# Reordering the set-up of a fused conv, state-space, attention and expert kernel

## The chip, the cores and the metric

The kernel runs on one core of a Trainium2 chip. The metric is the device time of one execution in microseconds (us), as the median of several runs. A core has TensorE (matmuls, PE in the profile), VectorE (DVE), ScalarE (ACT), GpSimd (POOL) and SyncE (SP). Transfers between device memory and on-chip memory (DMA) are issued from the queues of SyncE or ScalarE here and carried by 16 DMA engines.

## The reference, cut to what matters

The input x has 4 images of 128 channels and 64 x 64 pixels, in float32.

```python
x = x + conv_block(gn(x))           # layer 0
t = to_tokens(x)                    # (4, 4096, 128)
t = t + attention(ln(t))            # layer 1, 4 heads of 32
t = t + experts(ln(t))              # 8 experts, the best 2 of each token
out = from_tokens(t)

def gn(v, G=32, eps=1e-5):          # statistics over 4 channels and all pixels
    g = v.reshape(B, G, C // G, H, W)
    return ((g - mean(g)) / sqrt(var(g) + eps)).reshape(v.shape)

def conv_block(x):
    xn = ln(x)                                        # over channels
    h = depthwise_3x3(xn) + fc1_b
    y = xn + fc2(gelu(ln(h))) + fc2_b
    chunks = ln(y) split into 4 groups of 32 channels
    m = mamba(chunks) + skip * chunks                 # a scan over 4096 pixels, 16 states
    return ln(xn + cat(m)) @ proj_w.T + proj_b
```

Group normalisation needs the mean and variance of a whole image before its first block can be normalised. Some weights are prepared once. The expert and router weights and the projection are centred over the channels, so that the mean of a normalisation need not be subtracted later. Norms of the query, key and value weights bound the attention scores: the flag `general` says whether a slower general attention must run after all, which is decided at the kernel's end.

## The kernel before, in words

An image is cut into NB = 8 blocks of 512 pixels (8 rows of 64), with the 128 channels on the partitions. The kernel has two parts.

The **set-up** (L59 to L193) loads weights with `load` (L53 to L57), on SyncE's queue unless another is given, makes constants, prepares weights and computes the bound. Its order on each engine comes from a scheduler that follows the data and the order of the program. The tiles `taps` (nine diagonal matrices of the depthwise weights, L85 to L87), `inxc` (L90 to L93), `amat`, `wdt` and `crow` are made here. The pools `scratch` and `bound` are closed at its end, and the memory is given to the main pools.

The **main part** is written out by hand, in slots. The helper `Queue` (L467 is the line in it that records every operation of this part) chains the instructions of each engine in the order of the program. Work on blocks runs as generators in two lanes, X and Y, which `advance` moves on by one stage. `until` (L1246 on) runs the lanes until a named piece is done; it is what works off the first blocks, before slot 0 can start. For each image the lanes run:

- `group_norm(b)`: loads all eight blocks of the image (`xg`), takes bn_stats of each, then the group means with two small matmuls by `gmat`, and `gr`, the power -1/2 of the variance, on GpSimd;
- `first_norm(b, i)`: loads a block again (`gn`), normalises it with the group's mean `gm` and `gr`, transposes it, normalises each pixel over the channels (statistics on VectorE, power on GpSimd, scaling on ScalarE, the tile `xt`), transposes back and writes `y0` with a border; block i also writes the last border row of block i - 1;
- `conv(b, i)`: nine taps of the depthwise convolution (on TensorE for image 0, on VectorE for the others), normalisation, gelu, the matmul `fc2T`, the sum with y0, normalisation again, giving `xn`; then `pairs`, a shifted copy, goes through a transfer;
- `inputs(b, i, p)`: projections, silu and softplus for half p of the channels; it writes `bc` to memory, to be fetched as broadcast `rows`.

The slots of the main loop then run the scans on VectorE (`h`), read them out (`hc`), sum over states with transposing matmuls (`y`), and interleave attention (`sc`, `pT`, `av`) and experts (`share`).

```python
    mix, att, side = pool("mix"), pool("att"), pool("side")
...
    for k in range(2):
        gpsimd.memset(decays[k][:, 0, BLK:], 0.0)
```

The first statement lays out the main pools in memory. The memset (tile `da`) is the first instruction of the main part on GpSimd.

Of the kernel before, what the change touches and what calls it, by code (L numbers as in the profile page):

```python
# [9 lines left out]
F32 = mybir.dt.float32  # L10
# [26 lines left out]
def conv_mamba_attn_moe_kernel(ctx: ExitStack, tc: tile.TileContext, t: dict):  # L37
# [20 lines left out]

    ident = const.tile([P, P], F32, name="ident")  # L59
# [10 lines left out]
    gmat = load("gmat")  # L70
    lnw, lnb, lcw, lcb = (load(k) for k in ("lnw", "lnb", "lcw", "lcb"))
    fc1w, fc1b, fc2T, fc2b = (load(k) for k in ("fc1w", "fc1b", "fc2T", "fc2b"))
    inz, cb, dtb, dsk, wbc = (load(k) for k in ("inz", "cb", "dtb", "dsk", "wbc"))
    wout, projT = (load(k) for k in ("wout", "projT"))
    wv, wp, rw, ew, eb8 = (load(k, eng=nc.scalar) for k in ("wv", "wp", "rw", "ew", "eb8"))
    wqn, wkn, bqn, bkn = (load(k, eng=nc.scalar) for k in ("wqn", "wkn", "bqn", "bkn"))
# [3 lines left out]
    inx, xdt, dtT, alog = (load(k, pool=scratch) for k in ("inx", "xdt", "dtT", "alog"))  # L80
    bvc, bp = (load(k, pool=scratch) for k in ("bvc", "bp"))
    cw = load("cw", [P, 4, P], t["cw"].partition_broadcast(P), pool=scratch)
# [20 lines left out]
    with (  # L103
        tc.tile_pool(name="bound", bufs=1) as bd,
        tc.tile_pool(name="ps_w", bufs=2, space=PSUM) as ps_w,
    ):
# [3 lines left out]
        pw = ps_w.tile([P, P], F32, name="pw")  # L110
        nc.tensor.matmul(pw[0:1, :], lhsT=bvc, rhs=wp, start=True, stop=True)
        crow1 = bd.tile([1, C], F32, name="crow1")
        nc.vector.tensor_add(crow1, pw[0:1, :], bp)
        pw = ps_w.tile([P, P], F32, name="pw")
        nc.tensor.matmul(pw, lhsT=ones, rhs=crow1, start=True, stop=True)
        nc.vector.tensor_copy(crow, pw)

        sq = bd.tile([P, 2 * NH + 1], F32, name="sq")
        nc.vector.memset(sq, 0.0)
        bsq = bd.tile([DH, 2 * NH], F32, name="bsq")
        for i, (w, bias) in enumerate(((wqn, bqn), (wkn, bkn))):
            for h in range(NH):
                r = slice(DH * h, DH * h + DH)
# [516 lines left out]
    def conv(b, i):  # L643
        cm = tmp("Y", "cm")
        h = work("Y") if b == 0 else cm
        hr = h.rearrange(IMAGE, w=IMG)

        def tap(k):
            y0 = y0_rows(b, i, k // 3, k % 3)
# [837 lines left out]
```

## Time and profile before

| What | us |
|---|---|
| Median of 3 runs | 5233.21 (5232.01 to 5235.14) |
| The profiled execution's own time | 5221.24 |
| Its span in the profile | 5219.4 |
| PE busy | 4743.5 (91%) |
| VectorE busy | 3834.5 (73%) |
| ScalarE busy | 3749.8 (72%) |
| GpSimd busy | 423.5 (8%) |
| First scan input (`h`) starts at | 98.11 |

Busy times are of the profiled execution. PE's is an overestimate of its use, since its matmuls are pipelined and their ends modelled. Times in the timeline count from the start of the span. "Idle before" an instruction is followed by what released it. L467 stands for the whole main part, so its groups are told apart by the names of their tiles.

### The profile page before, as it was taken

What the parts mean: (1) busy time and instruction counts of PE and PEld (TensorE: products, weight loads), DVE (VectorE), ACT (ScalarE), POOL (GpSimd) and SP (SyncE); (2) the same over time, 40 slices, a digit from 0 to 9 for tenths busy, and PEclk for the clock granted to TensorE, in tenths of its full rate; (3) what the DMA queues carried; (4) which work ended last, traced back from release to release, by engine and by line L of the source; (5) the groups of instructions that cost most, each with busy time, mean ns of one, the idle gap of its engine ahead of it and who ended that gap; (6) DMA issues with size and microseconds to landing.
All of it is one profiled execution on the core that took longest, in us unless ns stands there. A gap on an engine that the chain in (4) does not pass through costs nothing.

```text
span 5219.4 us, 62693 instructions
## 1 busy us (share of the span) xinstructions
PE 4743.5 (91%) x20704; PEld 2300.7 (44%) x20704; DVE 3834.5 (73%) x5809; ACT 3749.8 (72%) x5701; POOL 423.5 (8%) x483
## 2 busy tenths in 40 slices
PE   4566898999999999899999999999999999999997
PEld 2333444444444444444444444444444444443443
DVE  4888767777788877888788877888788877751332
ACT  3456787788777777688887787788777787756543
POOL 1111101100000000001000000000000001000000
PEclk8677999999999999899999999999999999999998
DMA  3556667767776667767766667767766666754542
GB/s 96 188 186 202 206 215 247 232 231 238 244 231 218 227 227 243 238 232 246 260 230 231 224 223 230 262 227 259 259 236 227 215 230 226 263 181 153 184 134 72
DMA packets 451694, 1131.62 MB, mean 217 GB/s; under 512 B 51985, under 2 KB 135330, under 8 KB 451362
## 3 DMA queue, kind: packets, MB, share of 16 engines
q1 hardware_dynamic: 450194, 1126.74, 64.3%
q8 instruction: 166, 2.72, 0.2%
q14 instruction: 166, 1.36, 0.1%
q10 hardware_dynamic: 1168, 0.80, 0.1%
HBM read 967.12 MB, written 143.39 MB: 213 GB/s over the span
## 4 chain that ended last, share of the span: by engine, by line
PE 55%; DVE 18%; ACT 13%; DMA 6%; issue 5%; POOL 2%; SPq 1%; DVEq 0%; ACTq 0%; POOLq 0%
PE av L467 23%; PE sc L467 13%; PE ps_X L467 8%; DVE h L467 6%; PE ps_Y L467 5%; PE y L467 5%; ACT pT L467 4%; ACT L467 3%; DMA ks<-kd 2%; DVE hc L467 2%; ACT xt L467 1%; ACT e L467 1%; DMA rows<-bcd 1%; DVE stX L467 1%; POOL rsX L467 1%
## 5 line engine op out<-in xcount | busy, mean ns | idle before, releaser
L467 ACT ACTIVATE pT<-sc 128x1024 f32<-128x1024 f32 x2048 | 1984.8, 1023 | 940.1 <-PE sc L467 938.4
L467 PE MATMUL av<-pT,v 128*64 128x512 f32 x8192 | 1998.3, 609 | 12.4 <-DVE avs L467 12.4
L467 PE MATMUL sc<-qs,ks 128*128 128x512 f32 x4096 | 1296.1, 436 | 64.4 <-DMA ks<-kd 32.7
L467 DVE TENSOR_TENSOR_SCAN h<-da,state,h 128x1025 f32<-128x1025 f32 x512 | 1204.2, 2352 | 90.0 <-ACT h L467 56.2
L467 PEld LDWEIGHTS sc<-qs,ks 128*128 128x128 f32 x4096 | 701.3, 190 | 793.3 <-ACT pT L467 261.7
L467 PEld LDWEIGHTS av<-pT,v 128*64 128x64 f32 x8192 | 499.5, 137 | 844.4 <-issue 813.8
L467 ACT ACTIVATE da<-delta,amat 128x512 f32<-128x512 f32 x1024 | 743.0, 730 | 1.9
L467 PE MATMUL y<-ident,hc 128*128 128x128 f32 x4096 | 626.6, 284 | 64.9 <-DVE hc L467 64.9
L467 DVE TENSOR_TENSOR hc<-rows,h 128x1024 f32<-128x1024 f32 x512 | 624.2, 1219 | 16.1 <-PE y L467 5.9
L467 DVE TENSOR_TENSOR h<-rows,du 128x1024 f32<-128x1024 f32 x512 | 623.4, 1218 | 14.2 <-DMA rows<-bcd 13.7
L467 PEld LDWEIGHTS y<-ident,hc 128*128 128x128 f32 x4096 | 520.6, 147 | 235.7 <-issue 83.9
L467 ACT ACT_TABLE_LOAD x319 | 409.3, 1283 | 19.5 <-DVE zs L467 14.3
L467 POOL TENSOR_TENSOR rsX<-rsX,mhalf 128x4 f32<-128x4 f32 x92 | 203.8, 2216 | 2524.6 <-DVE rsX L467 2440.5
L467 POOL TENSOR_TENSOR rsY<-rsY,mhalf 128x4 f32<-128x4 f32 x100 | 130.4, 1304 | 2071.0 <-DVE shiftY L467 1560.3
L467 DVE TENSOR_TENSOR avs<-av,prev 128x512 f32<-128x512 f32 x96 | 66.1, 689 | 252.9 <-PE av L467 238.3
L467 PE MATMUL ps_X<-share,w_ew 128*128 128x512 f32 x432 | 215.5, 622 | 8.7 <-DVE share L467 8.5
L467 ACT ACTIVATE xt<-ps_Y,shiftY,rsY 128x128 f32<-128x128 f32 x380 | 143.8, 469 | 106.4 <-POOL shiftY L467 99.0
L467 DVE TENSOR_TENSOR share<-share,xf 128x1024 f32<-128x1024 f32 x128 | 155.9, 1218 | 15.6 <-DMA share<-sharesX 9.9
L467 ACT COPY state<-h 128x2 f32<-128x2 f32 x448 | 88.7, 198 | 93.5 <-DVE h L467 93.5
L467 DVE SCALAR_TENSOR_TENSOR cm<-y,w_fc1w,cm 128x512 f32<-128x512 f32 x192 | 142.8, 744 | 3.4
L467 PE MATMUL ps_Y<-pairs,inxc 128*128 128x512 f32 x256 | 129.2, 629 | 15.6 <-DMA pairs<-xn 10.3
L467 PEld LDWEIGHTS ps_X<-share,w_ew 128*128 128x128 f32 x432 | 73.6, 190 | 146.8 <-issue 98.5
(254 smaller groups left out, 3455.8 us busy)
## 6 DMA issues: line engine op xcount, KB each, us to landing
rows<-bcd SPq DMA_DIRECT2D x1024, 512.0 KB
ks<-kd SPq DMA_DIRECT2D x192, 512.0 KB
qs<-qd SPq DMA_DIRECT2D x161, 512.0 KB
share<-sharesX SPq DMA_DIRECT2D x108, 512.0 KB
v<-vd SPq DMA_DIRECT2D x192, 256.0 KB
ks<-kd SPq DMA_DIRECT2D x128, 256.0 KB
avd<-avs SPq DMA_DIRECT2D x96, 256.0 KB
prev<-avd SPq DMA_DIRECT2D x96, 256.0 KB
```

The lines of the kernel that those rows point to most:

```text
L467: return lambda *args, **kw: queued(op(*args, **kw))
```

## The change

- Eight tiles `x0` in `scratch` take the eight blocks of image 0; their loads are the first on SyncE's queue.
- All weights but `rb`, `skip` and `projb` are loaded from ScalarE's queue, in a new order. `bvc` and `bp` move from `scratch` to `const`.
- The group statistics of image 0 are computed in the set-up, from `x0`; `group_norm(0)` is no longer put into lane Y.
- The bound check, `crow` and the centring leave the set-up for a generator, `prepared_weights`. `until` moves it on by one stage per round once y0 of block 1 has been issued; what is left is run in slot 0. It works in a `pT` tile of the attention and in the PSUM tile `av`. The eight Gram matrices share one PSUM tile, as do their squares, and `ew` is centred in two matmuls of 512 columns instead of eight of 128.
- The convolution of block (0, 0) does taps 0 to 4 on TensorE and taps 5 to 8 on VectorE, and adds the two sums on VectorE.
- The pool `att` is opened ahead of `mix`.

```diff
--- before.py
+++ after.py
@@ -56,6 +56,12 @@
         eng.dma_start(out=w, in_=src)
         return w
 
+    x0 = []
+    for i in range(NB):
+        xs = scratch.tile([P, BLK], F32, name=f"x0{i}")
+        nc.sync.dma_start(out=xs, in_=x[0][:, i * BLK : (i + 1) * BLK])
+        x0.append(xs)
+
     ident = const.tile([P, P], F32, name="ident")
     make_identity(nc, ident)
     ones = const.tile([1, P], F32, name="ones")
@@ -67,19 +73,19 @@
     for e in range(NE):
         nc.gpsimd.memset(rev[:, e : e + 1], float(NE - e))
 
-    gmat = load("gmat")
-    lnw, lnb, lcw, lcb = (load(k) for k in ("lnw", "lnb", "lcw", "lcb"))
-    fc1w, fc1b, fc2T, fc2b = (load(k) for k in ("fc1w", "fc1b", "fc2T", "fc2b"))
-    inz, cb, dtb, dsk, wbc = (load(k) for k in ("inz", "cb", "dtb", "dsk", "wbc"))
-    wout, projT = (load(k) for k in ("wout", "projT"))
-    wv, wp, rw, ew, eb8 = (load(k, eng=nc.scalar) for k in ("wv", "wp", "rw", "ew", "eb8"))
-    wqn, wkn, bqn, bkn = (load(k, eng=nc.scalar) for k in ("wqn", "wkn", "bqn", "bkn"))
+    late = nc.scalar
+    gmat, fc1w = (load(k, eng=late) for k in ("gmat", "fc1w"))
+    inx, xdt, dtT, alog = (load(k, pool=scratch, eng=late) for k in ("inx", "xdt", "dtT", "alog"))
+    cw = load("cw", [P, 4, P], t["cw"].partition_broadcast(P), pool=scratch, eng=late)
+    lnw, lnb, fc1b, lcw, lcb = (load(k, eng=late) for k in ("lnw", "lnb", "fc1b", "lcw", "lcb"))
+    fc2T, fc2b, cb, dtb, dsk = (load(k, eng=late) for k in ("fc2T", "fc2b", "cb", "dtb", "dsk"))
+    inz, wbc, wout, projT = (load(k, eng=late) for k in ("inz", "wbc", "wout", "projT"))
+    wv, wp, rw, ew, eb8 = (load(k, eng=late) for k in ("wv", "wp", "rw", "ew", "eb8"))
+    wqn, wkn, bqn, bkn = (load(k, eng=late) for k in ("wqn", "wkn", "bqn", "bkn"))
+    bvc, bp = (load(k, eng=late) for k in ("bvc", "bp"))
     rb = load("rb", [P, NE], t["rb"].partition_broadcast(P))
     skip = load("skip", [P, 1], t["skip"].partition_broadcast(P))
     projb = load("projb", [P, C], t["projb"].rearrange("o c -> (o c)").partition_broadcast(P))
-    inx, xdt, dtT, alog = (load(k, pool=scratch) for k in ("inx", "xdt", "dtT", "alog"))
-    bvc, bp = (load(k, pool=scratch) for k in ("bvc", "bp"))
-    cw = load("cw", [P, 4, P], t["cw"].partition_broadcast(P), pool=scratch)
 
 
     taps = const.tile([P, 9, P], F32, name="taps")
@@ -100,96 +106,29 @@
 
     crow = const.tile([P, C], F32, name="crow")
     general = const.tile([1, 1], I32, name="general")
-    with (
-        tc.tile_pool(name="bound", bufs=1) as bd,
-        tc.tile_pool(name="ps_w", bufs=2, space=PSUM) as ps_w,
-    ):
+    with tc.tile_pool(name="ps_w", bufs=2, space=PSUM) as ps_w:
+        gst = small.tile([P, NB, 6], F32, name="gst", bufs=1)
+        for i in range(NB):
+            nc.vector.bn_stats(out=gst[:, i, :], in_=x0[i])
+        gmv = small.tile([P, 2], F32, name="gmv", bufs=1)
+        nc.vector.bn_aggr(out=gmv, in_=gst)
+        pw = ps_w.tile([P, P], F32, name="pw")
+        nc.tensor.matmul(pw[:, 0:1], lhsT=gmat, rhs=gmv[:, 0:1], start=True, stop=True)
+        gm0 = small.tile([P, 1], F32, name="gm", bufs=2)
+        nc.vector.tensor_copy(gm0, pw[:, 0:1])
+        gd = small.tile([P, 1], F32, name="gd", bufs=1)
+        nc.vector.tensor_sub(gd, gmv[:, 0:1], gm0)
+        gv = small.tile([P, 1], F32, name="gv", bufs=1)
+        nc.vector.scalar_tensor_tensor(gv, gd, gd, gmv[:, 1:2], ALU.mult, ALU.add)
+        pw = ps_w.tile([P, P], F32, name="pw")
+        nc.tensor.matmul(pw[:, 0:1], lhsT=gmat, rhs=gv, start=True, stop=True)
+        gr0 = small.tile([P, 1], F32, name="gr", bufs=2)
+        nc.vector.tensor_scalar_add(gr0, pw[:, 0:1], EPS)
+        nc.gpsimd.tensor_tensor(gr0, gr0, mhalf[:, 0:1], ALU.pow)
+
         pw = ps_w.tile([P, P], F32, name="pw")
         nc.tensor.matmul(pw, lhsT=xdt, rhs=dtT, start=True, stop=True)
         nc.vector.tensor_copy(wdt, pw)
-        pw = ps_w.tile([P, P], F32, name="pw")
-        nc.tensor.matmul(pw[0:1, :], lhsT=bvc, rhs=wp, start=True, stop=True)
-        crow1 = bd.tile([1, C], F32, name="crow1")
-        nc.vector.tensor_add(crow1, pw[0:1, :], bp)
-        pw = ps_w.tile([P, P], F32, name="pw")
...
-        for i, (w, bias) in enumerate(((wqn, bqn), (wkn, bkn))):
-            for h in range(NH):
-                r = slice(DH * h, DH * h + DH)
-                pw = ps_w.tile([P, P], F32, name="pw")
...
-        ok = bd.tile([1, 1], F32, name="ok")
-        nc.vector.tensor_reduce(ok, fine, AX.X, ALU.min)
-        nc.vector.tensor_scalar(ok, ok, -1.0, 1.0, ALU.mult, ALU.add)
-        nc.vector.tensor_copy(general, ok)
-        cen = bd.tile([P, P], F32, name="cen")
-        nc.vector.tensor_scalar(cen, ident, 1.0 / C, None, ALU.subtract)
-
-        def centred(w, src):
...
-        centred(rw, rw)
-        ewf = ew.rearrange("p e c -> p (e c)")
-        centred(ewf, ewf)
-        gain = bd.tile([P, C], F32, name="gain")
...
-        nc.vector.tensor_add(projb, pw, projb)
-        centred(projT, gain)
     setup.close()
@@ -501,7 +440,7 @@
             tc.tile_pool(name=name, bufs=bufs, **({} if space is None else {"space": space}))
         )
 
-    mix, att, side = pool("mix"), pool("att"), pool("side")
+    att, mix, side = pool("att"), pool("mix"), pool("side")
     ps_sc, ps_av, ps_y = pool("ps_sc", 2, PSUM), pool("ps_av", 1, PSUM), pool("ps_y", 1, PSUM)
     ps_work = pool("ps_work", 1, PSUM)
 
@@ -564,6 +503,7 @@
     held = set()
     group_of, y0_of, xn_of, pairs_of, in_of, gated, kqv = {}, {}, {}, {}, {}, {}, {}
     IMAGE = "p (r w) -> p r w"
+    group_of[0] = gm0, gr0
 
     def load_x(src, i, name):
         xs = side.tile([P, BLK], F32, tag="xs", name=name, bufs=4)
@@ -643,28 +583,34 @@
     def conv(b, i):
         cm = tmp("Y", "cm")
         h = work("Y") if b == 0 else cm
-        hr = h.rearrange(IMAGE, w=IMG)
+        half = b == i == 0
 
         def tap(k):
             y0 = y0_rows(b, i, k // 3, k % 3)
             w = fc1w[:, k : k + 1]
 
-            if b == 0:
-                mm(hr, taps[:, k, :], y0, k == 0, k == 8)
-            elif k == 0:
+            hr = (cm if half and k > 4 else h).rearrange(IMAGE, w=IMG)
+            if b == 0 and not (half and k > 4):
+                mm(hr, taps[:, k, :], y0, k == 0, k == (4 if half else 8))
+            elif k == 0 or half and k == 5:
                 vector.tensor_scalar(hr, y0, w, fc1b, ALU.mult, ALU.add)
             else:
                 vector.scalar_tensor_tensor(hr, y0, w, hr, ALU.mult, ALU.add)
 
-        for k in range(0, 9, 2):
+        for k in range(0, 5 if half else 9, 2):
             if b:
                 yield
             tap(k)
-            if k < 8:
+            if k < (4 if half else 8):
                 tap(k + 1)
+            if half and k < 4:
+                tap(k + 5)
+                tap(k + 6)
             if b == 0:
                 yield
-                if k == 8:
+                if half and k == 4:
+                    vector.tensor_add(cm, h, cm)
+                elif k == 8:
                     scalar.activation(cm, h, AF.Identity, bias=fc1b)
             yield
         ps = transposed("Y", by_tile(cm))
@@ -1209,6 +1155,99 @@
         yield
 
 
+    def prepared_weights():
+
+        kept_in = att.tile([P, 2, BLK], F32, name="pT", bufs=4).rearrange("p k q -> p (k q)")
+        column = [0]
+
+        def part(n, rows=P):
+            c = column[0]
+            column[0] += n
+            return kept_in[0:rows, c : c + n]
+
+        def bank():
+            return ps_av.tile([P, BLK], F32, name="av")
+
+        cen, gain, lnbs, gv = (part(P) for _ in range(4))
+        g, sq, bsq, col1 = part(2 * NH * DH, DH), part(2 * NH + 1), part(2 * NH, DH), part(1)
+        crow1 = part(C, 1)
+        norm, bnorm, power = part(2 * NH + 1, 1), part(2 * NH, 1), part(4 * NH, 1)
+        wn, most, score, fine, ok = (part(n, 1) for n in (2 * NH, 2 * NH, NH, NH + 1, 1))
+        heads = [
+            (NH * i + h, slice(DH * h, DH * h + DH), w, bias)
+            for i, (w, bias) in enumerate(((wqn, bqn), (wkn, bkn))) for h in range(NH)
+        ]
+        gpsimd.memset(power[:, 0 : 2 * NH], 0.125)
+        gpsimd.memset(power[:, 2 * NH :], 0.5)
+        vector.memset(sq, 0.0)
+        vector.memset(col1, 1.0)
+        vector.tensor_scalar(cen, ident, 1.0 / C, None, ALU.subtract)
+        ps = bank()
+        for k, r, w, _ in heads:
+            mm(ps[0:DH, DH * k : DH * k + DH], w[:, r], w[:, r])
+        mm(ps[0:1, 2 * NH * DH : 2 * NH * DH + C], bvc, wp)
+        yield
+        vector.tensor_copy(g, ps[0:DH, 0 : 2 * NH * DH])
+        vector.tensor_add(crow1, ps[0:1, 2 * NH * DH : 2 * NH * DH + C], bp)
+        yield
+        ps = bank()
+        for k, _, _, _ in heads:
+            c = slice(DH * k, DH * k + DH)
+            mm(ps[0:DH, c], g[:, c], g[:, c])
+        mm(ps[:, 2 * NH * DH : 2 * NH * DH + C], ones, crow1)
+        for k, r, _, bias in heads:
+            vector.tensor_copy(bsq[:, k : k + 1], bias[r, :])
+        vector.tensor_mul(bsq, bsq, bsq)
+        vector.tensor_mul(gv, wv, wv)
+        vector.tensor_reduce(sq[:, 2 * NH : 2 * NH + 1], gv, AX.X, ALU.add)
+        yield
+        vector.tensor_copy(g, ps[0:DH, 0 : 2 * NH * DH])
+        vector.tensor_copy(crow, ps[:, 2 * NH * DH : 2 * NH * DH + C])
+        vector.tensor_mul(g, g, g)
+        vector.tensor_reduce(
+            sq[0:DH, 0 : 2 * NH], g.rearrange("p (k d) -> p k d", d=DH), AX.X, ALU.add
+        )
+        yield
+        ps = bank()
+        mm(ps[0:1, 0 : 2 * NH + 1], col1, sq)
+        mm(ps[0:1, DH : DH + 2 * NH], col1[0:DH, :], bsq)
+        yield
+        vector.tensor_copy(norm, ps[0:1, 0 : 2 * NH + 1])
+        vector.tensor_copy(bnorm, ps[0:1, DH : DH + 2 * NH])
+        vector.tensor_scalar(
+            fine[:, NH : NH + 1], norm[:, 2 * NH : 2 * NH + 1], VALUE_MAX, None, ALU.is_le
+        )
+        yield
+        gpsimd.tensor_tensor(wn, norm[:, 0 : 2 * NH], power[:, 0 : 2 * NH], ALU.pow)
+        gpsimd.tensor_tensor(bnorm, bnorm, power[:, 2 * NH :], ALU.pow)
+        for k in range(0, NE * C, BLK):
+            ps = bank()
+            mm(ps, cen, ew.rearrange("p e c -> p (e c)")[:, k : k + BLK])
+            yield
+            vector.tensor_copy(ew.rearrange("p e c -> p (e c)")[:, k : k + BLK], ps)
+            yield
+        vector.tensor_scalar_mul(gain, projT, lnw)
+        vector.tensor_copy(lnbs, lnb.to_broadcast([P, P]))
+        yield
+        ps = bank()
+        mm(ps[:, 0:C], lnbs, projT)
+        mm(ps[:, C : 2 * C], cen, gain)
+        mm(ps[:, 2 * C : 2 * C + NE], cen, rw)
+        yield
+        vector.tensor_add(projb, ps[:, 0:C], projb)
+        vector.tensor_copy(projT, ps[:, C : 2 * C])
+        vector.tensor_copy(rw, ps[:, 2 * C : 2 * C + NE])
+        yield
+        vector.scalar_tensor_tensor(most, wn, 1.001 * float(C) ** 0.5, bnorm, ALU.mult, ALU.add)
+        vector.tensor_mul(score, most[:, 0:NH], most[:, NH:])
+        vector.tensor_scalar(fine[:, 0:NH], score, SCORE_MAX / ATT_SCALE, None, ALU.is_le)
+        vector.tensor_reduce(ok, fine, AX.X, ALU.min)
+        vector.tensor_scalar(ok, ok, -1.0, 1.0, ALU.mult, ALU.add)
+        vector.tensor_copy(general, ok)
+        yield
+
+    weights = prepared_weights()
+
     lanes, done, running = {"X": deque(), "Y": deque()}, set(), {}
 
     inside = {"X": False, "Y": False}
@@ -1251,6 +1290,8 @@
                 advance(*half) for half in (("X", True), ("Y", False), ("Y", True), ("X", False))
             ]
             assert any(moved) or len(done) > count, key
+            if ("y0", *blocks[1]) in done:
+                next(weights, None)
 
     blocks = [(b, i) for b in range(B) for i in range(NB)]
 
@@ -1262,7 +1303,7 @@
 
     def upper(k):
         b, i = blocks[k]
-        if i == 0:
+        if i == 0 and b > 0:
             Y.append((("group", b), group_norm(b), []))
         if k != 1:
             Y.append((("y0", b, i), first_norm(b, i, "Y"), before(k, 4)))
@@ -1326,6 +1367,8 @@
         flush()
         if slot == 0:
             fetch((0, 0), (0, 1), (1, 0))
+            for _ in weights:
+                pass
             prepared(0, 0)
             prepared(0, 1)
         fetch((at + 2, 0) if odd else (at + 1, 1))
```

## The prediction

> **What bounds the kernel now.** I read the busy times by stage first (columns: length, then busy time and instructions of matmul, weight load, VectorE, ScalarE and GpSimd; granted clock, DMA share, GB/s).
>
> ```profile
> 0.00:39.00 39.00, 14.23 (x68) 10.11 (x68) 19.29 (x98) 1.50 (x2) 5.62 (x24) 1.00 0.40 110
> 39.00:98.00 59.00, 28.04 (x64) 12.95 (x65) 10.50 (x48) 21.20 (x35) 5.65 (x17) 0.79 0.10 30
> 98.00:400.00 302.00, 176.68 (x658) 105.56 (x657) 266.08 (x330) 160.78 (x316) 36.55 (x36) 0.72 0.55 186
> ...
> 1000.00:2000.00 1000.00, 948.62 (x4270) 461.64 (x4267) 798.25 (x1152) 793.44 (x1217) 84.57 (x97) 0.99 0.70 233
> ```
>
> TensorE bounds the body (95% busy); VectorE, with the scans, bounds 98 to 400 us (88%). Neither bounds the first 98 us: there no engine is half busy, and time is latency. The change touches only this stretch. So the question is how much earlier the first scan's input (L467 h, 98.11 us) is ready, and whether all that follows moves with it. Then the timeline of the set-up (start, length, engine, instruction, idle before and releaser):
>
> ```profile
> 13.56 0.33 SPq L56 DMA_DIRECT2D w_cw<-in_cw  x1
> 13.94 9.61 SPq L467 DMA_DIRECT2D xg<-in_x  x8
> ...
> 17.84 1.19 DVE L93 TENSOR_TENSOR inxc<-w_inx,w_cw 64x128 f32<-64x128 f32 x4 [2.00 <-DMA w_cw<-in_cw]
> ...
> 27.59 0.35 DVE L467 BATCH_NORM_AGGREGATE gmv<-gst 128x2 f32<-128x48 f32 x1
> ...
> 33.12 0.14 DVE L467 TENSOR_SCALAR gr<-ps_Y 128x1 f32<-128x1 f32 x1
> ...
> 37.71 0.29 DVE L180 COPY w_projT<-pw 128x128 f32<-128x128 f32 x1
> 37.87 0.14 POOL L467 MEMSET da<- 128x1 f32 x2 [5.41 <-issue]
> 37.94 0.54 POOL L467 MEMSET vst<- 128x512 f32 x1
> 38.42 0.58 POOL L467 TENSOR_TENSOR gr<-gr,mhalf 128x1 f32<-128x1 f32 x1
> 39.04 0.55 DVE L467 TENSOR_SCALAR gn<-gn,gm,gr 128x512 f32<-128x512 f32 x1 [1.04 <-POOL gr L467]
> ...
> 43.87 1.50 ACT L467 ACTIVATE xt<-ps_Y,shiftY,rsY 128x128 f32<-128x128 f32 x4 [29.54 <-POOL shiftY L467]
> ```
>
> The rows of x are asked for only at 13.94, behind 26 weight loads on the SP queue. Their statistics are interleaved with the bound check on VectorE. The group variance is there at 33.26, but its power waits on GpSimd behind a memset that starts only when the last set-up tile is written (37.71 + 0.29). The first block can start at 39.0. The waits of the SP queue show that a load can hold up later issues:
>
> ```profile
> SPq L56 <- DMA w_ew<-in_ew: 1.4, 1, 1.4
> ```
>
> Last, the first block's convolution and what follows:
>
> ```profile
> 52.68 9.67 PE L467 MATMUL ps_Y<-y,taps 128*128 128x512 f32 x18
> ...
> 54.39 0.34 PEld L467 LDWEIGHTS ps_Y<-y,taps 128*128 128x128 f32 x1 [0.52 <-issue]
> ...
> 57.47 0.19 PEld L467 LDWEIGHTS ps_Y<-y,taps 128*128 128x128 f32 x1 [0.24 <-issue]
> ...
> 62.39 0.69 ACT L467 ACTIVATE cm<-ps_Y,w_fc1b 128x512 f32<-128x512 f32 x1 [8.39 <-PE ps_Y L467]
> ...
> 70.25 2.08 PE L467 MATMUL ps_Y<-g,w_fc2T 128*128 128x512 f32 x2 [0.98 <-ACT g L467]
> ```
>
> Each tap is two passes. Their weight loads come every 0.86 us (0.34 + 0.52) at first and every 0.43 us (0.19 + 0.24) from about 56.4 us on.
>
> **What the Trainium skill says.** "TensorE: Matmul & The Clock Gate", Part 1: the clock has a half and a full state and needs some 3.4 us of activity to rise. The 0.86 and 0.43 us passes agree, although the windows print 1.00 for the same time. "DMA: Bandwidth & Descriptors", section "Issuing engines are not separate DMA queues": loads issued by ScalarE and SP share the same DMA engines, so a second queue saves only issue time. The trace agrees with sharing: the 256 KB load of cw took 4.28 us (13.56 to 17.84) beside four x loads. "ScalarE: Activation LUTs", section "What ACT_TABLE_LOAD costs": 1283 ns; the trace has 1.28.
>
> **The change part by part.** *Order.* I compared the built programs by engine. From the first input projection (inxc) on, all five engines issue the same instructions in the same order in both, with the same waits but for the now unneeded or first-use waits on loads. The swap of the pools att and mix adds none: cost 0. What changes is the first 83 us.
>
> *Loads.* 45 loads precede the first pairs transfer in both (26 + 10 on SP and 9 on ScalarE; now 13 and 32). In the built program each waits for the load eight places before it, both queues counted together. An issue takes 0.46 us; a 64 KB load (wv) landed 2.0 us after its issue, and cw 4.28. For a 256 KB x load beside others I take 3.4 us, about the mean of both. x00 is issued at 0.75 as gmat was, and lands at 4.1. On ScalarE alog waits for it (4.1) and cw follows (4.6), landing at 8.9. x03 waits for gmat (2.8) and lands with the others' data at 7.5: four x loads and cw moved 1.28 MB between 15 and 20 us before, so about 1 us per 256 KB. x07 shares cw's place, goes at 8.9 and lands at 12.3. gn follows rb, skip and projb on SP and lands near 15: before it is needed.
>
> *Statistics.* VectorE's order now is four bn_stats, inxc, two bn_stats, nine taps, two bn_stats, aggregate. cw frees inxc at 8.9; then 1.19 (inxc) + 1.34 (2 x 0.67) + 1.85 (taps row) + 1.34 + 0.35 = 6.07 gives 15.0. x07 is needed at 13.95, after it lands. Then gmat's matmul 0.58, three small VectorE rows 0.73 (28.61 to 29.34), matmul 0.58, gr 0.14, power 0.58 and 0.24 for hand-overs: 2.85. The group's gr is ready at 17.8 instead of 39.0: **21.2 us earlier**. Ends: 16.2 if loads land as fast as wv did; 20.5 if each x load takes as long as cw.
>
> *The ScalarE queue.* xt is wanted 4.87 us after gr (43.87 - 39.0), so at 22.7. dtb is the 16th of 32 loads and waits for x07 (12.3); it and the 16 after it at 0.46 end at 20.1; table load 1.28 and amat 0.22 make 21.6. So it hides, by 1.1 us. If the big loads hold the queue as ew held SP (1.4 us each, for ew, wout and cw), ScalarE is 3.1 us late: cost 0 to 3.1, I take 0.
>
> *Convolution* (times of before, from y0 on). PE first does eight 32x32 matmuls and a row: a pair of passes was 0.32 us alone, some 0.2 in a stream: 1.8 us, so taps start at 54.4. Slow clock until 56.2 (two passes), six passes at 0.43: 58.8. Then eight g matmuls and crow, 1.6; the fifth tap 0.86 and its drain: 61.4. VectorE meanwhile does tap 5 (0.55), waits for block 1's row (54.0), then tap 6, g, crow, taps 7 and 8, bsq, gv: 0.74 + 0.33 + 0.28 + 1.49 + 1.1 + 0.7 ends at 58.7, so it is covered by PE. The sum, a 0.7 us add, ends at 62.1 instead of 63.08: 1.0 saved. If the small matmuls take 0.32 each, 2 us of this go back; if PE is warm from the first tap, 1 more is won.
>
> *Check and centring in the gaps.* g, crow, square and reduction (0.33 + 0.29 + 0.33 + 0.3) stand ahead of the next bn_stats and overlap the 0.66 us transposes: +0.5. One 512-wide ew matmul precedes fc2T while ScalarE makes g: at 1.72 to 2.08 from 69.2 it ends at 70.9 or later against 70.25: +0.6. It may leave PE warm, so that fc2T's 2.08 falls by up to 0.8: I take -0.6. The w_ew copies, the second ew matmul, the last three matmuls and the small VectorE rows lie under transposes (1.12), GpSimd's power and xt (4.3 together), and the 2.3 us pairs transfer: 0. Were that last cover gone, they would cost about 2 us. GpSimd's two powers (1.67 + 1.63) come after shift and 9 us before the next one: 0.
>
> Sum: 21.2 + 1.0 - 0.5 - 0.6 + 0.6 = 21.7, rounded to **21.5 us** earlier. The body keeps its order and its waits, so nothing refills the gap; what is late next is still the scan chain, only earlier. The span would go from 5219.4 to 5197.9 and the profiled execution from 5221.24 to 5199.7. The median of the runs lies 12.0 above that execution, taken as unchanged: 5233.2 - 21.5 = **5211.7**.
>
> **Rivals.** *The ScalarE queue sets the start* (10%): 32 loads in one queue, with waits crossing to SP. For: the margin is 1.1 us and SP stalled 1.4 us on ew. Against: most of these loads are small. Gain 21.5 - 6 = 15.5 at twice the stalls: 5217.7.
>
> *TensorE gains too* (8%): the extra matmuls leave it at full clock for the taps, fc2T and inxc, two matmuls of which took 3.57 us at 83.72 where 1.72 is warm. For: PE now works in the gaps. Against: idle stretches of 2 to 4 us remain. Gain 21.5 + 0.8 + 1.8 + 2 = 26: 5207.
>
> *The head was hidden anyway* (4%): the body would wait for something not moved. For: the scans run at 88% of VectorE, not 100. Against: the chain of waits runs without a break from gn through y0, taps, xn and pairs to h. It would give 5230, inside 0.2%.
>
> *Slower: the clock sinks between 98 and 400 us* (4%). In the first 300 us matmuls of ps_Y, ps_X and y are 16.9 + 4.0 + 2.7% of the chain, 71 us, at a mean of 0.72. Loss cancels the gain where 71 x (0.72/c - 1) = 21.5, at c = 0.55; at a steady half clock it is 31 us and the time 5243. For: the windows show 0.50 at 70 to 80 and at 180 to 200 us. Against: the work between is the same.
>
> **How the numbers follow.** The main case has 74%, with its own range 5207 to 5217 from the ends of loads and convolution. Both neighbours of same sign are needed for eight in ten with margin: 5204 to 5220. About 0.2% (10.5 us) is what a measurement can tell from no change; faster by more needs half of the forecast gain, which the first three cases give: 0.92. Hidden head 0.04, slower 0.04.
>
> **What would show it.** bn_stats from about 4.5 us; the aggregate near 14.6; gr's power ending at 17 to 19; xt near 22.7; taps in two groups on PE and four rows on VectorE, the add ending near 41; the first scan input h near 76.5; every later stage shifted alike. It is wrong if the last ScalarE load is issued after 22 us, if inxc waits past 11 us for cw, if the fifth tap waits on VectorE, or if the shift at h is not the shift at the end.

## The result, and the profile after

The changed kernel took 5215.75 us (median of 6 runs, 5212.52 to 5219.71), beside 5237.89 us (6 runs, 5232.01 to 5245.92) for the kernel before. The ratio is 0.9967, with a 95% interval of 0.9954 to 0.9979: faster by 17.3 us of 5233 (11.0 to 24.1). The forecast was 21.5 us of gain and 5211.7 us. Its profiled execution took 5213.97 us with a span of 5211.8.

First the busy times by stage of the changed kernel. The stages are the same pieces of work as in the table shown for the kernel before: up to the group's power, up to the first scan input, the next 302 us, and one millisecond of the body (columns as there: length, PE, PEld, VectorE, ScalarE, GpSimd, granted clock, DMA share, GB/s).

```profile
0.00:19.50 19.50, 1.89 (x6) 1.50 (x6) 9.22 (x26) 0.00 (x0) 2.23 (x20) 1.00 0.73 183
19.50:78.40 58.90, 31.22 (x106) 15.54 (x107) 21.14 (x91) 22.09 (x36) 8.95 (x20) 0.79 0.17 43
78.40:380.00 301.60, 179.16 (x657) 106.32 (x655) 263.32 (x329) 158.90 (x313) 36.88 (x36) 0.72 0.55 185
1000.00:2000.00 1000.00, 946.58 (x4276) 460.14 (x4276) 797.39 (x1142) 796.19 (x1219) 83.23 (x96) 0.99 0.70 233
```

The first stage shrank from 39.0 to 19.5 us: VectorE now does 26 instructions in it instead of 98, and DMA runs at 0.73 of its engines instead of 0.40. The second stage kept its length (58.9 against 59.0) although VectorE has twice the work in it. The last two stages are unchanged.

The timeline of the changed kernel's head (start, length, engine, instruction, idle before and releaser):

```profile
5.06 0.36 ACTq L56 DMA_DIRECT2D w_cw<-in_cw  x1
...
10.78 1.19 DVE L99 TENSOR_TENSOR inxc<-w_inx,w_cw 64x128 f32<-64x128 f32 x4 [2.58 <-DMA w_cw<-in_cw]
...
16.25 0.37 DVE L114 BATCH_NORM_AGGREGATE gmv<-gst 128x2 f32<-128x48 f32 x1
...
18.90 0.57 POOL L127 TENSOR_TENSOR gr<-gr,mhalf 128x1 f32<-128x1 f32 x1 [16.66 <-DVE gr L126]
...
19.50 0.55 DVE L406 TENSOR_SCALAR gn<-gn,gm,gr 128x512 f32<-128x512 f32 x1 [0.76 <-POOL gr L127]
...
22.30 0.30 ACTq L56 DMA_DIRECT2D w_bp<-in_bp  x1
...
23.93 0.21 ACT L102 ACTIVATE amat<-w_alog 128x16 f32<-128x16 f32 x1
...
24.34 1.51 ACT L406 ACTIVATE xt<-ps_Y,shiftY,rsY 128x128 f32<-128x128 f32 x4 [0.20 <-POOL shiftY L406]
...
34.70 4.54 PE L406 MATMUL ps_Y<-y,taps 128*128 128x512 f32 x8
...
35.72 0.34 PEld L406 LDWEIGHTS ps_Y<-y,taps 128*128 128x128 f32 x1 [0.52 <-issue]
...
36.51 0.19 PEld L406 LDWEIGHTS ps_Y<-y,taps 128*128 128x128 f32 x1 [0.45 <-issue]
...
36.94 0.19 PEld L406 LDWEIGHTS ps_Y<-y,taps 128*128 128x128 f32 x1 [0.24 <-issue]
...
40.20 1.13 PE L406 MATMUL ps_Y<-y,taps 128*128 128x512 f32 x2
...
41.37 0.69 DVE L406 TENSOR_TENSOR cm<-ps_Y,cm 128x512 f32<-128x512 f32 x1 [2.30 <-PE ps_Y L406]
...
50.21 1.91 PE L406 MATMUL ps_Y<-g,w_fc2T 128*128 128x512 f32 x2
...
78.44 1.23 DVE L406 TENSOR_TENSOR h<-rows,du 128x1024 f32<-128x1024 f32 x1
```

The statistics' chain is closed: inxc waits 2.58 us for cw, and from there to gr's power there is nothing but work and the hand-overs between engines. GpSimd takes the power as soon as its input is there; the memset `da` now runs at 1.66 us, long before. ScalarE is only just ready for xt: its last load is issued at 22.30, amat ends at 24.14, and xt starts at 24.34, released by GpSimd. The shift of each stage against the kernel before:

| Stage | Before | After | Shift | Forecast of the shift |
|---|---|---|---|---|
| gr's power ends | 39.00 | 19.47 | 19.5 | 21.2 |
| sum of the taps ends | 63.08 | 42.06 | 21.0 | 22.2 |
| fc2T starts | 70.25 | 50.21 | 20.0 | 21.1 |
| first inxc matmul starts | 83.72 | 63.58 | 20.1 | 21.7 |
| first scan input h starts | 98.11 | 78.44 | 19.7 | 21.7 |

The two profiled executions, though, differ by only 7.6 us in span (5219.4 and 5211.8). The first experiment shows why they can't be compared at their ends.

### The profile page after: what moved, and what is told of

Same layout as the page of the kernel before. It is cut to its first block, busy times and chain, and to the rows that moved or that the text cites. A ratio compares the mean times of both kernels' runs of the same rounds, so it can differ in the third digit from the quotient of the medians.

```text
span 5211.8 us, 62608 instructions
## 1 busy us (share of the span) xinstructions
PE 4743.5 (91%) x20684; PEld 2298.3 (44%) x20684; DVE 3834.8 (74%) x5780; ACT 3749.6 (72%) x5700; POOL 423.0 (8%) x483
## 4 chain that ended last, share of the span: by engine, by line
PE 56%; DVE 17%; ACT 13%; DMA 6%; issue 5%; POOL 2%; SPq 1%; DVEq 0%; ACTq 0%; POOLq 0%
PE av L406 23%; PE sc L406 13%; PE ps_X L406 9%; DVE h L406 6%; PE ps_Y L406 5%; PE y L406 5%; ACT pT L406 4%; ACT L406 3%; DMA ks<-kd 2%; DVE hc L406 2%; ACT xt L406 1%; ACT e L406 1%; DMA rows<-bcd 1%; POOL rsX L406 1%; DVE stX L406 1%
## 5 line engine op out<-in xcount | busy, mean ns | idle before, releaser
L406 ACT ACT_TABLE_LOAD x319 | 409.3, 1283 | 19.5 <-DVE zs L406 14.3
L406 DVE TENSOR_TENSOR share<-share,xf 128x1024 f32<-128x1024 f32 x128 | 155.9, 1218 | 20.5 <-DMA share<-sharesX 14.8
```

The costliest lines, as they stand in the source:

```text
L406: return lambda *args, **kw: queued(op(*args, **kw))
```

## The experiments

"h" below is the start of the first scan input, read from one profile of each kernel. "Time" is the mean of the runs less the mean of the runs of the kernel before on the same chip; the ratio has its 95% interval.

One profile fixes h only to some 3 us. The changed kernel was profiled four times and gave 78.4, 80.6, 81.4 and 78.8, although its first inxc matmul started at 62.9 to 63.7 in all four. The difference lies in three matmuls that follow it. Two of them, in the first profile:

```profile
67.23 1.12 PE L406 MATMUL ps_X<-xn,w_inz 64*128 64x512 f32 x2
...
70.05 1.13 PE L406 MATMUL ps_Y<-xin,wdt 128*128 128x512 f32 x2
```

And in the third:

```profile
67.42 2.07 PE L406 MATMUL ps_X<-xn,w_inz 64*128 64x512 f32 x2
...
72.08 2.07 PE L406 MATMUL ps_Y<-xin,wdt 128*128 128x512 f32 x2
```

At about half the speed they put h 17.7 us behind the first inxc matmul, at full speed 14.9 to 15.3. Below, "late h" marks a profile in which they ran slowly. Both profiles of the kernel before (14.4) and the first of the changed kernel ran them fast, so the shift of 19.7 us compares like with like.

**Does a shorter head reach the end?** One theory is the forecast's: the body moves with the head, one to one. The rival: the profiled pair shows what happens, most of the 19.7 us fades inside the body. Two kernels are the changed one with 36 and 108 multiplications by 1.0 of the last rows of x ahead of their bn_stats, which alter no value and only delay the head; two are the kernels before and after unaltered.

```diff
         for i in range(NB):
+            if i == NB - 1:
+                for _ in range(36):      # 108 in the longer one
+                    nc.vector.tensor_scalar_mul(x0[i], x0[i], 1.0)
             nc.vector.bn_stats(out=gst[:, i, :], in_=x0[i])
```

The kernel before again:

> The kernel before, unchanged, to have a second profiled execution of it. Theory R (the head's gain moves everything after it alike): between this profile and that of the changed kernel the scans' starts differ by 19.7 us at the first one (98.1 against 78.4 us) and by 15 to 25 us at the last one; the first profile of before was a fast execution by chance, and this one's span is near 5231 us. Theory F (the body takes part of the gain back in fixed places, between 280 and 1100 us): the difference fades again from 19.7 to 10 or less in the same places, and the span is near 5219 us.

The changed kernel again:

> The changed kernel, unchanged, timed beside before on one chip. Theory R: 19 to 22 us faster than before, ratio 0.9959 to 0.9964. Theory F: 8 to 12 us faster, ratio 0.9977 to 0.9985.

36 multiplications:

> The changed kernel, with the last block of image 0 multiplied by 1.0 in place 36 times on VectorE ahead of its bn_stats: 36 x 0.55 = 20 us more ahead of the group statistics, all else as in the changed kernel. Theory R: first scan input near 98.5 us, and the time equals that of before, within 3 us (some 20 us above the changed kernel). Theory F: only 8 us or so above the changed kernel, 10 us or more below before.

108 multiplications:

> The same with 108 multiplications, 108 x 0.55 = 59.5 us. Theory R: 59 us above the changed kernel, 39 us above before (ratio 1.0075). Theory F: some 25 us above the changed kernel, so about 5 us above before (ratio 1.001).

Measured: the multiplications took 0.46 us each, not the 0.55 expected, so the delays are 17 and 50 us. The shorter one, h at 95.2, ran in 1.0002 (0.9993 to 1.0010) of the time before; the longer one, h at 130.4, in 1.0063 (1.0048 to 1.0078). The changed kernel again had 0.9963 (0.9950 to 0.9976). Between the two delays h moved by 35.2 us and the mean time by 32.5. The kernel before, profiled once more, started its scans 0.7 us later than in its first profile and ended its last one 17.0 us later: the same program. Its 19 runs beside these spread from 5225.22 to 5242.83. So the fading seen in the first pair is the wander of single executions, and with the two delays the rival falls.

**What is each part worth?** Four kernels undo parts of the change. In the first, all nine taps of block (0, 0) are on TensorE:

```diff
-        half = b == i == 0
+        half = False
```

> The changed kernel with one part undone: all nine taps of block (0, 0) run on TensorE and ScalarE adds the bias. By the forecast (split worth 1.0 us): h starts 1.0 us later than after the change, the time 1 us longer, which the runs can't tell from nothing. By a recount of the trace after (four taps in 4.54 us at half clock and with the small matmuls ahead, the fifth in 1.13): the small matmuls stay ahead of the taps and the four taps that return cost 4 x 0.86 = 3.4 us at the slow clock or 1.7 at the fast one, less the 0.3 of the fifth tap's wait, so h starts 1.5 to 3.5 us later. If TensorE gains speed from a longer unbroken stream, below 1.5. The body shifts by the same amount.

h came at 84.3 (late h) instead of the 78.4 to 81.4 of the changed kernel's four profiles; time -15.6, ratio 0.9970 (0.9958 to 0.9983). The timeline of this kernel:

```profile
34.95 5.30 PE L406 MATMUL ps_Y<-y,taps 128*128 128x512 f32 x8
...
41.21 3.70 PE L406 MATMUL ps_Y<-y,taps 128*128 128x512 f32 x8
...
45.09 1.13 PE L406 MATMUL ps_Y<-y,taps 128*128 128x512 f32 x2
46.25 0.69 ACT L406 ACTIVATE cm<-ps_Y,w_fc1b 128x512 f32<-128x512 f32 x1 [11.54 <-PE ps_Y L406]
```

The four taps that came back take 3.70 us at full clock, and the sum ends at 46.94 instead of 42.06. Against the two profiles of the changed kernel with a late h the split is worth 3 to 4 us of the head, and as much at the first inxc matmul (66.97 against 62.9 to 63.7); the time doesn't resolve it. Its worth in the forecast, 1.0, was against the kernel before and already paid for the check's small matmuls ahead of the taps.

In the second, the check, crow and the centring are back in the set-up, with loads, statistics and pool order as changed; in the third the pools are also in the old order; in the fourth only the pools are. No run keeps the old loads with all else changed, so the share of the early rows isn't measured by itself.

```diff
# second and third
+        sq = bd.tile([P, 2 * NH + 1], F32, name="sq")
...
+        centred(projT, gain)
     setup.close()
...
-    weights = prepared_weights()
+    weights = iter(())
# third and fourth
-    att, mix, side = pool("att"), pool("mix"), pool("side")
+    mix, att, side = pool("mix"), pool("att"), pool("side")
```

> The changed kernel with the bound check, crow and centring put back into the set-up; loads, statistics and the pool order stay as changed. If moving the check was worth nothing by itself (rows first and power first do it all): gr's power still ends near 19.5 us, and h starts within 2 us of 78.4 to 80.6. If the check stands in the way where it was: its some 50 small VectorE rows and 40 matmuls, which were 39.0 - 27.6 = 11 us of the set-up before, fall between 19.5 and 35 us, VectorE and TensorE are shared with first_norm of blocks 0 and 1, and h starts 5 to 11 us later, with the time longer by the same.

> As the kernel with the check back in the set-up, but the pools opened in the old order (mix ahead of att), so that GpSimd's first tile of the main part lies where the set-up's tiles lay. The forecast put the order of the pools at 0. If that is right in general: the same h as with the check back alone. If the order is what frees GpSimd from the end of the set-up: the memset da waits for the last set-up tile, the power of the first block's pixels waits behind it, and h starts 5 us or more later than with the check back alone, 10 to 20 us later than after the change; that would give back nearly all of the gain although rows and statistics come early.

> The changed kernel with nothing undone but the order of the two pools (mix ahead of att again). If the order counts only because of the check's tiles (9.5 us at h with the check in the set-up: 97.1 against 87.6): the memset da waits only for the last reader of the first scratch tiles, at most until amat ends near 24.2, the power of the first block's pixels then comes 0 to 3 us late, and h starts at 78 to 83 us. If the order is worth about the same by itself: h at 87 to 90. The forecast said 0.

With the check back, gr's power ended at 19.33, as in the changed kernel, but h came at 87.6 (late h), 6 to 7 us after the changed kernel's late ones: time -10.2, ratio 0.9981 (0.9973 to 0.9989). Its Gram matrices and their VectorE rows stand between the transposes and the normalisation of block 1: xt of block 1 starts at 35.48 instead of 30.68. With the old pool order too, h came at 97.1 (not a late one; the first inxc matmul moved by 12.5 us, from 69.91 to 82.41) and the gain was gone: time +5.3, ratio 1.0006 (0.9997 to 1.0016). Its timeline:

```profile
42.94 0.29 DVE L205 COPY w_projT<-pw 128x128 f32<-128x128 f32 x1
43.10 0.14 POOL L492 MEMSET da<- 128x1 f32 x2 [5.61 <-issue]
...
43.65 1.04 POOL L492 TENSOR_TENSOR rsY<-rsY,mhalf 128x4 f32<-128x4 f32 x1
...
45.00 1.51 ACT L492 ACTIVATE xt<-ps_Y,shiftY,rsY 128x128 f32<-128x128 f32 x4 [20.75 <-POOL shiftY L492]
```

The group's power is done at 19.39, but the next power on GpSimd, that of the first block's pixels, stands behind the memset `da`, which starts only with the last copy of the set-up (at 1.74 in the kernel that differs by the pool order alone). ScalarE waits 20.75 us for it. It is the wait that the forecast read in the kernel before, moved by one instruction. And it is not only the check that holds the memset. With nothing but the pool order undone:

```profile
24.99 0.21 ACT L102 ACTIVATE amat<-w_alog 128x16 f32<-128x16 f32 x1
...
25.27 0.13 POOL L406 MEMSET da<- 128x1 f32 x2 [4.91 <-ACT amat L102]
...
25.82 1.02 POOL L406 TENSOR_TENSOR rsY<-rsY,mhalf 128x4 f32<-128x4 f32 x1
...
27.15 1.50 ACT L406 ACTIVATE xt<-ps_Y,shiftY,rsY 128x128 f32<-128x128 f32 x4 [1.95 <-POOL shiftY L406]
```

Here the memset waits for amat, and amat comes behind ScalarE's 32 loads. From gr's power to xt it takes 6.79 us instead of 4.87 to 4.95. The first inxc matmul starts 2.0 us later than in the changed kernel beside it (65.69 against 63.73) and h 1.6 us later (83.1 against 81.4, both late). The times, -18.8 and ratio 0.9962 (0.9949 to 0.9975), can't tell this from nothing.

**Can the head be shortened further, and does that still count?** The first further version lets VectorE take all statistics first, makes taps and inxc later, and loads ten weights behind the first `gn` loads on SyncE's queue.

```diff
-    inx, xdt, dtT, alog = (load(k, pool=scratch, eng=late) for k in ("inx", "xdt", "dtT", "alog"))
+    xdt, dtT, alog = (load(k, pool=scratch, eng=late) for k in ("xdt", "dtT", "alog"))
...
-    for k in range(9):
-        nc.vector.tensor_scalar_mul(taps[:, k, :], ident, fc1w[:, k : k + 1])
...
         gn = load_x(x[b], i, "gn")
+        if (b, i) == (0, 1):
+            for k in TAIL:               # wqn wkn bqn bkn bvc bp ew eb8
+                sync.dma_start(out=tail[k], in_=t[k])
+            sync.dma_start(out=inx, in_=t["inx"])
+            sync.dma_start(out=cw, in_=t["cw"].partition_broadcast(P))
...
+        for k in range(9):               # first in prepared_weights
+            vector.tensor_scalar_mul(taps[:, k, :], ident, fc1w[:, k : k + 1])
```

> The changed kernel taken further: VectorE does the eight bn_stats first, with taps and inxc made afterwards in its idle time; inx, cw and eight weights that nothing needs early are loaded on SyncE's queue behind the first gn loads, so that ScalarE issues 22 loads instead of 32. If the statistics set the start: aggregate at about 11.6 instead of 16.25 (x07's landing or eight rows of 0.67 from 4.5 on), gr's power at about 14.9 instead of 19.5, h 4.5 us earlier than after the change, and the time about 4.5 us shorter. If ScalarE's queue still sets it (amat ends later than gr + 4.9) or the loads that moved stand before gn: less than 2 us. If the taps now come late for the first convolution: h unchanged or later.

h came at 74.9: gr's power ended at 15.78 (15.21 + 0.57), 3.7 us earlier than in the changed kernel. Ratio 0.9964 (0.9951 to 0.9978), time -16.7. It was run again beside the changed kernel:

> The changed kernel itself, on the same chip as the next three: h at 78 to 81 us and a time some 19 us under before, as in its two earlier runs. It is what the others of this call are held against.

> Statistics first and ten loads behind the first gn loads, as run before, now beside the changed kernel: h at 75, 4 to 5 us earlier than it. If the head passes to the end one to one, its time is 4 to 5 us below that of the changed kernel, which five rounds can hardly tell from nothing; a time above the changed kernel's by more than 5 us would say that the body doesn't move with the head.

h came at 81.4 and 77.5 (both late), the times at -20.8 (0.9962, 0.9950 to 0.9975) and -20.8 (0.9962, 0.9949 to 0.9976). Like with like the head is 3 to 4 us shorter each time; these runs don't show it in the time.

The second step fills idle stretches of TensorE with nine matmuls whose result nobody reads.

```diff
+    def warm(src, n):
+        sc = ps_sc.tile([P, 2, BLK], F32, name="sc")
+        for _ in range(n):
+            mm(sc[:, 0, :], ident, src)
...
         ps = transposed(lane, by_tile(gn))
+        if (b, i) == (0, 1):
+            warm(gn, 3)
...
         ps = transposed("Y", by_tile(cm))
+        if half:
+            warm(cm, 3)
...
+        if b == i == 0:                  # after the transposes that give xn
+            warm(cm, 3)
```

On top of the first step:

> As the one before, with nine matmuls of 128x512 added on TensorE whose result nobody reads: three after the first transposes of block 1, three after those of the first convolution's sum, three after the transposes that give xn. They fill idle stretches of 3 to 4 us ahead of the taps, of fc2T and of inxc. If TensorE's half clock in the head comes from its idle stretches: the four taps take 2.2 to 3.0 us instead of 4.2, fc2T some 1.0 instead of 1.91, the first inxc some 1.8 instead of 3.57, and h starts 3 to 6 us earlier, at 69 to 72. If the clock stays low all the same: the added matmuls only stand in the way, and h starts 0 to 2 us later than 75.

The timeline of this kernel:

```profile
24.28 4.24 PE L401 MATMUL sc<-gn,ident 128*128 128x512 f32 x6
30.49 3.70 PE L401 MATMUL ps_Y<-y,taps 128*128 128x512 f32 x8
35.15 1.13 PE L401 MATMUL ps_Y<-y,taps 128*128 128x512 f32 x2
37.55 2.74 PE L401 MATMUL sc<-cm,ident 128*128 128x512 f32 x6
44.63 1.12 PE L401 MATMUL ps_Y<-g,w_fc2T 128*128 128x512 f32 x2 [0.58 <-ACT g L401]
52.53 3.77 PE L401 MATMUL sc<-cm,ident 128*128 128x512 f32 x6
56.72 1.96 PE L401 MATMUL ps_Y<-pairs,inxc 128*128 128x512 f32 x4
...
69.50 1.23 DVE L401 TENSOR_TENSOR h<-rows,du 128x1024 f32<-128x1024 f32 x1
```

The first inxc takes 1.96 us; in every kernel built from the changed one without the added matmuls it took 3.57 to 3.75. The four taps take 3.70, less than the 4.22 to 5.58 without, but more than the 2.2 to 3.0 expected. fc2T's 1.12 says little by itself, since without the added matmuls it took anything from 1.16 to 2.08. So it was the idle stretches that kept the clock low ahead of the taps and of inxc. h came at 69.5, 11.9 us before the changed kernel beside it, but the time at -21.2, ratio 0.9959 (0.9946 to 0.9972): only 0.4 us less. Whether the body gives gains back below some start was tried with three more:

> The changed kernel once more, as the yardstick of the next two on one chip: h at 78 to 82 us.

> The changed kernel with the nine idle-filling matmuls alone (loads and statistics as changed). The two parts of the further step should add: of the 12 us at h (81.4 to 69.5), about 4 came from the statistics and 8 from TensorE's clock, so h at 72 to 75. If the head passes to the end one to one: 6 to 8 us below the changed kernel beside it. If the end no longer follows below an h of some 80 us: within 2 us of it.

> Both parts again, h at 69 to 70. One to one: 10 to 12 us below the changed kernel beside it, ratio to before near 0.9943. If the end no longer follows: within 3 us of the changed kernel, ratio near 0.996, as in its first runs (0.9959).

h came at 78.8, 73.6 and 69.5; the times at -16.9, -22.3 and -26.9; the ratios 0.9962 (0.9949 to 0.9974), 0.9953 (0.9940 to 0.9966) and 0.9951 (0.9937 to 0.9965). Here the end follows. A straight line through all fifteen kernels (change of the mean time against change of h from 98.4 us, weighted by the number of runs; standard errors) is 2.0 (±1.2) us + 1.01 (±0.07) x the change of h. Its slope rests on the four kernels with h from 88 to 130 us. The two runs of the last kernel lie 6.1 and 0.4 us above the line, the changed kernel's four from 5.5 below to 1.0 above, and the eleven kernels with h below 85 us alone have a slope of only 0.45 (±0.16). Part of that is h itself, which swings by 3 us from profile to profile: against the start of the first inxc matmul the slope of the eleven is 0.68 (±0.24). So one to one is shown down to the changed kernel; whether the last 10 us of the head reach the end in full stays open. The line would make the last kernel some 10 us faster than the changed one, the flatter slope 5; its own two comparisons gave 0.4 and 10.0 us, and their intervals overlap those of the changed kernel. It has the lowest ratio of all and beats the kernel before by 0.41 to 0.49%.

## Where the prediction held, and which of its steps failed

The mechanism of the forecast held: a chain of latencies, shortened at its start, moves the end. Two steps of its sum failed. The landing of cw was taken 1.9 us too early, and the body was to refill nothing but gave back 2.0 to 2.6 us.

*Right: what bounds the head, and the path.* The statistics and GpSimd's power did set the start, and every stage up to h moved alike, 19.5 to 21.0 us. That the head of the change reaches the end one to one was shown by the delays and by the line. The rival of a hidden head falls with that, and so does a fall of the clock as large as the slower case had it: the granted clock between the first scan input and 302 us later is 0.72 in both kernels.

*Mis-sized: the landing of cw.* The step "cw follows (4.6), landing at 8.9" measured 5.06 and 10.78: 5.72 us for 256 KB instead of the 4.28 taken from the trace of before (5.4 to 6.1 in the four profiles of the changed kernel, 4.28 and 4.29 in the two of before). In both kernels four x loads were issued close around it (at 4.33 to 6.25 here, at 13.94 to 15.4 there), but in the changed one three more had gone out at 0.75 to 1.67, and DMA was at 0.90 of its engines while cw was under way, against 0.63. What makes the 1.4 us was not isolated. All that follows in this step holds: from cw to the end of the aggregate 5.84 us (6.07 forecast), from there to gr's power 2.85 (2.85). gr came at 19.47, not 17.8, inside the ends of 16.2 to 20.5. So the 1.9 us that cw came late, less 0.2 won behind it, are the 1.7 us that gr's power missed. The version with the statistics first fits the term, with gr's power at 15.78, but it takes the rows of inxc and taps (1.19 + 1.84) out of the chain together with the wait for cw (2.58).

*Too early by 2.5 us, at almost no cost: the ScalarE queue.* It was to be free at 21.6, 1.1 us ahead of xt. It was free at 24.14: x07, for which dtb waits, went out only with cw's landing at 10.78, so dtb was issued at 13.82 instead of 12.3, and the loads from it on took 1.0 us more than their 0.46 us each. The last load was issued at 22.30, after the 22 us that the forecast had named as a sign of being wrong. The cost stayed near 0 because gr, and with it xt, was late by cw as well: xt waited for GpSimd, 0.20 us after the queue was free. In two other profiles of the changed kernel xt started without any idle time; the gap from gr to xt was 4.87 and 4.95 us there against 4.87, so the queue cost 0.1 us at most. That it cost no more was in part luck.

*Right sign: the convolution.* The taps' sum gained 1.5 us beyond the start (1.0 forecast). TensorE's slow clock held for some three of the eight passes: in the timeline of the section on the result their weight loads come every 0.86 us (0.34 + 0.52) up to 36.5 us and every 0.43 us (0.19 + 0.24) from then on.

From the sum to h 1.3 us went again (21.0 to 19.7), where the forecast had 0.5: fc2T stayed at 1.91 behind the check's ew matmul, and inxc at 3.73. The forecast let fc2T win 0.6. The rival "TensorE gains too" did not come about; the filled kernels show that it could.

*Wrong as it stood: "The swap of the pools att and mix adds none: cost 0".* It adds no wait, as said. What the step missed is that it takes one away: undone, it costs some 2 us of the head by itself, and 12.5 at the first inxc matmul with the check in the set-up. The forecast's number didn't suffer, since its sum had no wait on GpSimd between gr and xt anyway.

*Wrong: "The body keeps its order and its waits, so nothing refills the gap".* From the first scan to the 32nd it took 203.0 and 203.1 us in the two profiles of before, and 205.1 to 205.7 in the four of the changed kernel. All of it, and a little more, is lost between the 29th and the 31st scan: that stretch takes 15.7 us in both profiles of before, 18.5 in the four. TensorE there, in the second profile of before:

```profile
284.24 1.96 PE L467 MATMUL ps_Y<-pairs,inxc 128*128 128x512 f32 x4 [2.22 <-DMA pairs<-xn]
286.13 1.12 PE L467 MATMUL ps_X<-xn,w_inz 64*128 64x512 f32 x2
287.18 0.66 PE L467 MATMUL y<-ident,hc 128*128 128x128 f32 x4
287.94 1.07 PE L467 MATMUL ps_X<-xin,w_wbc 128*64 128x512 f32 x2
```

And in the changed kernel (its third profile):

```profile
266.15 2.52 PE L406 MATMUL ps_Y<-pairs,inxc 128*128 128x512 f32 x4 [2.23 <-DMA pairs<-xn]
268.60 2.07 PE L406 MATMUL ps_X<-xn,w_inz 64*128 64x512 f32 x2
270.60 1.11 PE L406 MATMUL y<-ident,hc 128*128 128x128 f32 x4
271.64 1.97 PE L406 MATMUL ps_X<-xin,w_wbc 128*64 128x512 f32 x2
```

The same matmuls in the same order, released alike, run at about half the speed, so the next inputs come later and VectorE waits. It is the forecast's slower rival in small: one stretch of clock lost, 2.6 us in the first pair of profiles, 2.0 to 2.6 in all. The constant of the line, 2.0 (±1.2), fits it, but is too uncertain to show it.

*The sum.* Head 19.7, less 2.6 in the body, is 17.1; the ratio gives 17.3 (11.0 to 24.1), the three repeats (0.9963, 0.9962, 0.9962) 19 to 20. The median of 5215.75 lies 4.05 above the forecast, inside the range of 5204 to 5220. The interval of the gain holds the forecast's 21.5 too, so the times alone don't show that the sum was too large. The traces do: at h the shift is 2.0 us below the 21.7 of the sum, 1.7 of it from gr's power, and 2.6 more go at the 30th scan. The step from span to median, "The median of the runs lies 12.0 above that execution, taken as unchanged", was wrong in itself. It put the profiled execution at 5199.7, and that took 5213.97: the 12.0 belonged to a short execution of before (the second profile of before lay 0.2 below its neighbours' median), and the changed kernel's median lay 1.8 above its own. It cancelled out, as the 5233.21 was a median and not that execution.

## What to carry to other kernels

A set-up whose engines are all half idle is a chain of latencies: follow it back from the first useful result, and look for the instruction of the main part that stands, by memory reuse or by order on its queue, behind the whole of the set-up. Moving inputs forward gains nothing while one such instruction remains: with rows and statistics early, but the check in the set-up and the pools in the old order, nothing was left of the gain. Judge a change of the head by a stage marker in the trace, chosen ahead of the places where the clock wavers (h was good to 3 us here, the first inxc matmul to 0.8), and by several executions for the end, since single executions of one program differed by up to 28.6 us (5198.35 to 5226.92).

## What the runs showed of the hardware that was not expected

- TensorE's half clock costs more of a latency-bound head than its busy time tells. The Trainium skill, "TensorE: Matmul & The Clock Gate", Part 1, says that the clock falls back after some 3.4 us of idleness and that the window in which activity is counted runs freely. The traces agree as far as they go. Ahead of the second inxc TensorE was idle for 5.3 to 5.6 us in every profile, and that inxc took 3.5 to 3.8 us, where 1.96 is the fast one. And the same program is slow in different places from one execution to the next: in four profiles the first four taps took 4.54, 5.58, 5.40 and 4.74 us and fc2T 1.91, 1.49, 1.39 and 1.91. The 3.4 us itself is shown by no run here. With nine matmuls added in idle stretches the head became 5.2 to 8.0 us shorter (78.8 to 73.6; 77.5, a late h, to 69.5).
- The loss at the 30th scan showed in all fifteen profiles of kernels built from the changed one (18.1 to 18.5 us from the 29th to the 31st scan), also where h was at 130.4, and in neither of the two of before (15.7). Undoing the split of the taps, the pool order, or the check with the pool order did not remove it. A freely running window would let it come and go, as the late h does; why it did not is open.
- A load of 256 KB beside others took 5.72 us where 4.28 had been read from the kernel before, though four x loads were issued close around it both times. Here DMA was at 0.90 of its engines while it was under way, there at 0.63.
